# Four fused pre-norm layers on one core: the last block's convolution wholly on TensorE, transposes of h moved within six frames, and a scatter issued later

## The chip, the cores and the metric

The kernel runs on one core of a Trainium2 chip. The metric is device time in microseconds for one execution. Before the change the median of 3 runs is 1512.05 us (1512.02 to 1517.49).

The engines are named as in the profile: PE is TensorE (PEld its weight loads), DVE is VectorE, ACT is ScalarE, POOL is GpSimd, SP is the engine that issues most transfers. Each runs its own instructions in program order; they wait for one another through semaphores.

## The reference, cut to what matters

The input x has 8 blocks of 512 rows of 128 numbers, all fp32. Four layers follow one another, each adding an attention part and a feed-forward part, and every part reads the layernorm of x:

```python
for part in (L0_attn, L0_ffn, L1_attn, L1_ffn, L2_attn, L2_ffn, L3_attn, L3_ffn):
    x = x + part(layernorm(x), weights)
```

The change touches the tail of layer 1's feed-forward part and what comes after. In layer 1, 256 chosen rows go through one expert of eight; their result is put back to their places (in the kernel, by a scatter into a tensor `back` in memory, and for block 0 by a product with a one-hot matrix). Layer 2 is attention with 16 heads of 64 over the 512 rows of each block, and then, for the first two blocks only, low-rank experts. Layer 3 is

```python
def L3_attn(x):                       # 21 taps per channel, causal
    c = sum(table[i] * shifted(x, i) for i in range(1, 21))   # table[0] is 0
    return x @ W1 + c @ W2 + bias
def L3_ffn(x):
    q = lambda a: fp4_round(a / scale(a)) * scale(a)   # scale by blocks of 16
    h = silu(q(x) @ q(w_gate).T) * (q(x) @ q(w_up).T)  # 352 wide
    return q(h) @ q(w_down).T
```

## The kernel before, in words

The residual x stays on chip, one tile of 128 partitions x 4 x 128 per block. The order of instructions on every engine is written out by hand (`manual_schedule`); the tile framework only adds the waits.

**The seam of layers 1 and 2.** `layer1` ends with a list of calls (lines 1178 to 1254). `chosen_out` makes `val`, the result of the chosen rows; `chosen_back` (line 1128) issues two indirect DMAs on POOL's queue that scatter `val` into `back`. The normalisations next to it, `z_stats(7)` and `stats_of(x[0])`, each end with three POOL instructions: add epsilon (line 243), power -1/2 (line 244), and the product with the mean (line 708). `z_out_by_three` adds a product to the residual on POOL (line 956) through one buffer `zo`. `xn` is layer 2's first normalised block; four transposes and a copy make `xt` of it, and `queries(0)` (line 1462) reads that. `keep_clock(n)` (line 765) issues n products that nobody reads.

**Frames.** `late` runs 64 frames, 8 to a block; frame n is two heads of layer 2's attention. In the main loop (line 2014) a frame is: `scores(n, 0)` (two tiles of products of k and q, their maxima on DVE, exponentials on ACT), `context(n - 1)`, `scores(n, 1)`, `queries(n + 2)`, `output(n - 1)`, `values(n + 1)`. Work of other layers hangs in the frames through four hooks: "P" after the first tile's exponentials of `scores(n, 0)` and, on PE, ahead of `context`; "V" just after; "G" between the halves; "E" at the frame's end. `planned(b, f0)` lays layer 3 of block b over 16 frames, from frame 8b + 8 (9 more than 8b for the first two blocks). Its parts are the convolution (`conv_v` on DVE, `conv_s` on ACT and POOL, `join`, then `conv_out` on PE), a second normalisation, the fp4 rounding of x (`quant_x1`, `quant_x2`), `turn_x`, the gate and up products (`gated`) with the rest of silu on DVE (`gated_v`), the rounding of h (`quant_h1`, `quant_h2`), its transposes (`turn_h`) and `down`. `turn_h(0)` hangs in "E", `turn_h(1)` a frame later in "P".

**PSUM.** Eight banks: two pairs (tag "two", used by scores), one each for contexts ("c") and the attention's output ("o"), and two single ones (tag "one") that queries, transposes, convolutions and `down` take in turn. A bank is taken again only when its last reader is done.

**The end.** The last block, 7, has no frames of layer 2 to hide in. `end` (line 1916) writes out an order of its own: block 6 (L) is finished from `gated` on, and block 7 goes through layer 3 in two halves of 256 rows, A and B. Of their 20 taps 12 are done on PE by products with `tap_w`, W2 with its rows scaled by one tap; taps 13 to 16 are on DVE and 17 to 20 on ACT and POOL. The weights `tap_w` are made by ACT, one per frame, in hook "G" from frame 25 on (line 1911). The two roundings of h share one buffer each for scale and values.

Of the kernel before, what the change touches and what calls it, by code (L numbers as in the profile page):

```python
# [160 lines left out]
def body(ctx, tc, dram, spans, x_in, ib, it, ic, ei, out):  # L161
# [84 lines left out]
    def mm(out_, lhs, rhs, start=True, stop=True):  # L246
        nc.tensor.matmul(out_, lhs, rhs, start=start, stop=stop)  # L247
# [534 lines left out]
    def layer1():  # L782
# [9 lines left out]
        with tc.tile_pool(name="l1", bufs=2) as wp, tc.tile_pool(name="l1c", bufs=1) as once:  # L792
# [145 lines left out]
            def z_turn(b):  # L938
                z_turned(t[b]["zn"], b % 2, J)
# [219 lines left out]
            with tc.manual_schedule():  # L1159

                nc.scalar.activation(
                    stat.tile([P, J], F32, tag="nb", name="nb")[:, :1], half[:, :1], AF.Exp
                )
                for zt in zts:
                    nc.gpsimd.memset(zt[64:65, :], 1.0)
                nought = once.tile([P, J, D], F32, tag="nought", name="nought")
                nc.gpsimd.memset(nought, 0.0)
                for b in range(1, NB):
                    nc.sync.dma_start(
                        back[b * TB : (b + 1) * TB, :].rearrange("(j p) d -> p j d", p=P), nought  # L1170
                    )
# [194 lines left out]
    def late():  # L1366
# [11 lines left out]
        with tc.tile_pool(name="a2", bufs=2) as wp, tc.tile_pool(name="l3", bufs=1) as lp:  # L1378
# [252 lines left out]

            pad = 20

            turned_taps = tuple(range(1, 13))
            tap_w = {}

            def tap_weights():
                w = lp.tile([P, 4, TB], F32, tag="cg", name="tapw")
                for k, i in enumerate(turned_taps):
                    tap_w[i] = w[:, k // 4, (k % 4) * P : (k % 4 + 1) * P]  # L1640
# [21 lines left out]
            def layer3(b, xp, tile_, part=(0, J), conv_bank="one", h_tag="h"):  # L1662
# [37 lines left out]
                def conv_p(*taps):  # L1700

                    t["conv"] = ps = bank(conv_bank)
                    for j in range(j0, j1):
                        for i in (0, *taps):
                            mm(
                                cols(ps, j),
                                xp()[:, pad - i + j * P : pad - i + (j + 1) * P],
                                tap_w[i] if i else l3["w1"],
                                start=(j == j0 and i == 0),
                                stop=False,  # L1710
                            )

                def join():
                    nc.vector.tensor_tensor(t["acc"], t["acc"], t["acs"], ALU.add)
# [44 lines left out]
                def gated(j):  # L1759

                    h = tile_("h", h_tile)
                    if whole:
                        pg, pu = bank(), bank()
                    else:
                        two = bank2()
                        pg, pu = two[:, 0, :], two[:, 1, :]
                    mm(pg[:, :I3], cols(t["xt"], j - j0), wt["gate"])
                    mm(pu[:, :I3], cols(t["xt"], j - j0), wt["up"])
                    s = lp.tile([P, I3], F32, tag="s", name="s", bufs=2)
                    nc.scalar.activation(s, pg[:, :I3], AF.Tanh, scale=0.5)  # L1770

                    def rest():
                        nc.vector.scalar_tensor_tensor(s, s, 1.0, pg[:, :I3], ALU.add, ALU.mult)
                        nc.vector.scalar_tensor_tensor(
                            h[:, j, :], s, 0.5, pu[:, :I3], ALU.mult, ALU.mult
                        )

                    t["rest", j] = rest

# [59 lines left out]
            def planned(b, f0_):  # L1839
# [26 lines left out]
                for j in range(J):  # L1866
# [49 lines left out]
            def end():  # L1916
# [14 lines left out]
                L.gated(0)  # L1931
                A.scale()
                L.gated_v(0)
                A.turn_()
                L.gated(1)
                B.scale()
                L.gated_v(1)
                B.turn_()
                L.gated(2)
                A.conv_p(*turned_taps)  # L1940
                A.conv_v(*range(13, 17))
                A.conv_s(*range(17, 21))
                L.gated_v(2)
                L.gated(3)
                B.conv_p(*turned_taps)
                L.quant_h1(0)
                B.conv_v(*range(13, 17))
                B.conv_s(*range(17, 21))
                A.join()
                A.conv_out()  # L1950
                A.stats2()
                L.gated_v(3)
                L.quant_h2(0)
                B.join()
                A.scale2()
                B.conv_out()
                B.stats2()
                A.quant_x1()
                A.quant_x2()
                L.turn_h(0)  # L1960
                B.scale2()
                L.quant_h1(1)
                A.turn_x()
                A.gated(0)
                A.gated(1)
                B.quant_x1()
                B.quant_x2()
                A.gated_v(0)
                A.gated_v(1)
                B.turn_x()  # L1970
                L.quant_h2(1)
                A.quant_h1(0)
                B.gated(2)
                B.gated(3)
                B.gated_v(2)
                A.quant_h2(0)
                L.turn_h(1)
                B.gated_v(3)
                L.down()
# [4 lines left out]
                A.down()  # L1984
                B.turn_h(1)
                B.down()

# [89 lines left out]
```

## Time and profile before

| | us |
|---|---|
| median of 3 runs | 1512.05 |
| the profiled execution | 1515.83 |
| its span, first to last instruction | 1514.0 |
| first scores of frame 0 | 560.44 |
| scores of frame 63 | 1427.34 |
| last add of the end | 1510.50 |

A frame is 11.12 to 16.75 us long, without experts; a block of 8 frames takes 103.04 us in the middle of the run. In an answer of the timeline, a line gives start, duration, engine, source line, operation, tiles (out<-in), shapes and count; "[0.42 <-DVE k L1471]" says that the engine was idle for 0.42 us just before, and what ended it. Durations of instructions in a pipeline overlap a little. PEclk is the granted clock of TensorE as a share of full speed.

### The profile page before, as it was taken

The page shows a single profiled execution, that of the slowest core. Times are in us where ns is not written, and L with a number is a line of the kernel's source. Part 1 is how long each engine was busy: PE and PEld are TensorE (multiplying, and loading weights), DVE is VectorE, ACT ScalarE, POOL GpSimd, SP SyncE. Part 2 cuts the span into 40 slices and gives each one's busy share as a digit, 9 for nine tenths or more (in the row PEclk, how much of TensorE's full clock was granted, in tenths as well). Part 3 has the DMA queues.
Part 4 walks back from the last instruction along what each step waited for, and adds up shares of the span by engine and source line. Part 5 has one row for each costly group of instructions (what it writes and reads, how often), then busy time and mean ns, then how long its engine had stood idle before and what let it go on. Part 6 is the DMA issues. An engine that isn't in the chain of part 4 may idle for free.

```text
span 1514.0 us, 22178 instructions
## 1 busy us (share of the span) xinstructions
PE 1408.5 (93%) x7670; PEld 671.8 (44%) x7670; DVE 1004.4 (66%) x2087; ACT 1049.5 (69%) x2141; POOL 648.3 (43%) x752
## 2 busy tenths in 40 slices
PE   7789999998789989999999999999999999999975
PEld 3652222222367654443443445445444444454554
DVE  6776777767466526552673486786777777867857
ACT  6869999888767446664875575876866767767621
POOL 6647666665655332310530172452532533514432
PEclk9999999999999799999999999999999999999986
DMA  5049999977331010001000000000000000000000
GB/s 181 1 60 133 130 126 129 129 116 102 86 132 32 15 39 22 22 0 27 2 1 1 0 1 8 1 2 7 1 1 8 1 8 1 1 8 1 1 7 15
DMA packets 32898, 58.90 MB, mean 39 GB/s; under 512 B 5522, under 2 KB 25554, under 8 KB 28307
## 3 DMA queue, kind: packets, MB, share of 16 engines
q1 hardware_dynamic: 32080, 55.66, 21.4%
q10 hardware_dynamic: 578, 1.57, 0.3%
q8 instruction: 61, 1.00, 0.3%
q14 instruction: 51, 0.41, 0.1%
q0 software_dynamic: 128, 0.26, 0.1%
HBM read 49.18 MB, written 8.29 MB: 38 GB/s over the span
## 4 chain that ended last, share of the span: by engine, by line
PE 65%; ACT 13%; DVE 13%; DMA 4%; POOL 2%; issue 2%; SPq 0%; POOLq 0%; DVEq 0%; ACTq 0%
PE ps L247 62%; ACT hm L556 4%; ACT ex L1498 3%; DMA gs<-gates 2%; ACT hm L555 2%; DVE nm L1492 2%; DMA gates<-eq 1%; DVE pr L568 1%; POOL rs L244 1%; DVE s L1402 1%; DVE fm L1299 1%; DVE fa L1300 1%; DVE fa L1301 1%; DVE s L703 1%; ACT xn L714 1%
## 5 line engine op out<-in xcount | busy, mean ns | idle before, releaser
L1498 ACT ACTIVATE ex<-ps,nm 128x512 f32<-128x512 f32 x512 | 345.4, 686 | 189.0 <-DVE nm L1492 182.2
L1492 DVE TENSOR_REDUCE nm<-ps 128x2 f32<-128x1024 f32 x256 | 300.4, 1215 | 71.4 <-PE ps L247 71.4
L247 PE MATMUL ps<-q,k 64*128 64x512 f32 x1024 | 256.7, 617 | 5.4 <-ACT ex L1498 4.5
L247 PE MATMUL ps<-ex,vs 128*64 128x512 f32 x1024 | 233.8, 599 | 0.0
L574 POOL TENSOR_TENSOR acc<-acc,pr 128x512 f32<-128x512 f32 x119 | 166.1, 1396 | 108.6 <-DVE pr L568 103.3
L1513 POOL TENSOR_TENSOR vs<-v,sm 128x256 f32<-128x256 f32 x128 | 81.3, 635 | 306.0 <-DVE sm L1512 283.0
L556 ACT ACTIVATE hm<-ps,blob_f 128x1536 f32<-128x1536 f32 x128 | 196.3, 1533 | 0.0
L247 PE MATMUL ps<-xt,blob_a 128*128 128x512 f32 x304 | 152.8, 629 | 0.0
L247 PE MATMUL ps<-h,w 32*128 32x512 f32 x1024 | 148.0, 639 | 3.4 <-DVE eq L467 1.8
L247 PEld LDWEIGHTS ps<-q,k 64*128 64x128 f32 x1024 | 87.2, 186 | 136.8 <-issue 67.8
L247 PE MATMUL ps<-hm,w 128*32 128x512 f32 x1024 | 136.4, 605 | 11.6 <-DVE pr L568 10.8
L568 DVE SCALAR_TENSOR_TENSOR pr<-ps,blob_f,gs 128x512 f32<-128x512 f32 x120 | 89.8, 748 | 73.8 <-PE ps L247 58.7
L1698 POOL TENSOR_TENSOR acs<-acs,prod 128x512 f32<-128x512 f32 (+1 forms) x104 | 128.9, 1240 | 16.7 <-ACT prod L1697 11.9
L247 PEld LDWEIGHTS ps<-ex,vs 128*64 128x64 f32 x1024 | 67.9, 136 | 151.9 <-issue 133.8
L555 ACT ACTIVATE hm<-ps,blob_f 128x512 f32<-128x512 f32 x128 | 88.0, 687 | 29.4 <-PE ps L247 29.3
L1498 ACT ACTIVATION_READ_ACCUMULATOR ex<-ps,nm 128x1 f32 x512 | 104.4, 204 | 0.0
L243 POOL TENSOR_SCALAR rs<-mv 128x4 f32<-128x4 f32 (+1 forms) x69 | 17.6, 254 | 202.5 <-DVE mv L1404 142.5
L247 PEld LDWEIGHTS ps<-xt,blob_a 128*128 128x128 f32 x304 | 53.3, 194 | 87.6 <-issue 66.5
L247 PEld LDWEIGHTS ps<-h,w 32*128 32x128 f32 x1024 | 40.9, 183 | 111.6 <-ACT hm L555 86.1
L1460 DVE TENSOR_TENSOR v<-ps,blob_bc 128x512 f32<-128x512 f32 x64 | 44.2, 690 | 65.8 <-PE ps L247 42.7
L247 PEld LDWEIGHTS ps<-blob_a,ct 128*128 128x128 f32 x512 | 67.0, 192 | 32.3 <-issue 29.2
L244 POOL TENSOR_TENSOR rs<-rs,half 128x4 f32<-128x4 f32 (+1 forms) x69 | 72.3, 1047 | 5.8
(295 smaller groups left out, 2230.3 us busy)
## 6 DMA issues: line engine op xcount, KB each, us to landing
gs<-gates SPq DMA_DIRECT2D x256, 128.0 KB
blob_f<-in_f SPq DMA_DIRECT2D x1, 2560.0 KB
blob_a<-in_a SPq DMA_DIRECT2D x1, 2056.0 KB
x<-in_x SPq DMA_DIRECT2D x8, 256.0 KB
gates<-eq SPq DMA_DIRECT2D x8, 256.0 KB
by_rows<-fxn SPq DMA_DIRECT2D x8, 256.0 KB
ge<-gates SPq DMA_DIRECT2D x4, 512.0 KB
back<-nought SPq DMA_DIRECT2D x7, 256.0 KB
```

Of the source, the lines that this page charges most:

```text
L243: nc.gpsimd.tensor_scalar(t, var, EPS, None, ALU.add)
L244: nc.gpsimd.tensor_tensor(t, t, half[:, : t.shape[-1]], ALU.pow)
L247: nc.tensor.matmul(out_, lhs, rhs, start=start, stop=stop)
L555: nc.scalar.activation(hm[:, 0, :], p1, AF.Gelu, bias=bias)
L556: nc.scalar.activation(hm[:, 1:, :], p3, AF.Gelu, bias=bias)
L568: nc.vector.scalar_tensor_tensor(pr, po, f0["b2"][:, e : e + 1], gs, ALU.add, ALU.mult)
L574: nc.gpsimd.tensor_tensor(acc[:, b, :], acc[:, b, :], pr, ALU.add)
L1460: nc.vector.tensor_tensor(v, pv, bias, ALU.add)
L1492: nc.vector.tensor_reduce(nm, ps, AX.X, ALU.max, negate=True)
L1498: nc.scalar.activation(ex[kt][:, i, :], ps[:, i, :], AF.Exp, bias=nm[:, i : i + 1], accum_out=sm[:, kt, i : i + 1],)
L1513: nc.gpsimd.tensor_tensor(vs[:, tiles, :, :], vs_[n][:, tiles, :].rearrange("p j (i n) -> p j i n", i=2), sm[:, tiles, :].unsqueeze(3).to_ ...
L1698: nc.gpsimd.tensor_tensor(t["acs"], t["acs"], p, ALU.add)
```

## The change

Five things are altered.

1. In `layer1`, `chosen_back()` is called after `stats_of(x[0])` and no longer before `z_stats(7)`.
2. `turn_h(0)` hangs in hook "P" of its frame, and no longer in "E". This concerns six blocks, 0 to 5; block 6's frames after the last one are dropped in favour of `end`.
3. `turned_taps` has all 20 taps. Eight more weights are made by ACT, in frames 37 to 44, in a new tile `tapx` (the last four).
4. In `end`, `conv_tile` does all taps and the W1 product of one tile of 128 rows in a row on PE, 21 products a tile; `conv_v`, `conv_s`, `join` and `conv_out` aren't called there any more. The order of `end` is new, with three `keep_clock`.
5. In `gated` for A and B, ACT copies half of the up product to SBUF, and POOL makes the last product of h from it; L's still runs on DVE. L's gate and up products take a "two" pair in `end`.

```diff
                 chosen_out()
-                chosen_back()
                 z_stats(7)
...
                 by = stats_of(x[0], J)
+                chosen_back()
                 z_turn(6)
...
-            turned_taps = tuple(range(1, 13))
+            turned_taps = tuple(range(1, 21))
...
+                def conv_tile(j):
+
+                    if j == j0:
+                        t["conv"] = bank(conv_bank)
+                    for i in (0, *turned_taps):
+                        mm(
+                            cols(t["conv"], j),
+                            xp()[:, pad - i + j * P : pad - i + (j + 1) * P],
+                            tap_w[i] if i else l3["w1"],
+                            start=(j == j0 and i == 0),
+                            stop=(j == j1 - 1 and i == turned_taps[-1]),
+                        )
...
+                    if at_end and thirds:
+                        u = block("prod", 3)()[:, :I3]
+                        nc.scalar.activation(u, pu[:, :I3], AF.Copy, scale=0.5)
...
+                        if at_end and thirds:
+                            nc.gpsimd.tensor_tensor(h[:, j, :], s, u, ALU.mult)
...
-                    (z + 5, "E", lambda: s.turn_h(0)),
+                    (z + 5, "P", lambda: s.turn_h(0)),
```

The order of calls in `end` after the two `stats`, before and after (g is `gated`, gv `gated_v`, kc `keep_clock`):

```
before: L.g0 A.scale L.gv0 A.turn_ L.g1 B.scale L.gv1 B.turn_ L.g2 A.conv_p A.conv_v A.conv_s L.gv2 L.g3
        B.conv_p L.quant_h1(0) B.conv_v B.conv_s A.join A.conv_out A.stats2 L.gv3 L.quant_h2(0) B.join
        A.scale2 B.conv_out B.stats2 A.quant_x1 A.quant_x2 L.turn_h(0) B.scale2 L.quant_h1(1) A.turn_x
        A.g0 A.g1 B.quant_x1 B.quant_x2 A.gv0 A.gv1 B.turn_x L.quant_h2(1) A.quant_h1 B.g2 B.g3 B.gv2
        A.quant_h2 L.turn_h(1) B.gv3 L.down B.quant_h1 A.turn_h B.quant_h2 (two tiles) A.down B.turn_h B.down
after:  L.g0 L.g1 A.scale A.turn_ L.gv0 B.scale L.g2 L.gv1 B.turn_ L.g3 A.conv_tile x2 L.quant_h1(0) L.gv2
        L.quant_h2(0) L.gv3 L.quant_h1(1) A.conv_added A.stats2 L.turn_h(0) L.quant_h2(1) B.conv_tile x2
        A.scale2 A.quant_x1 A.quant_x2 B.conv_added B.stats2 A.turn_x A.g0 B.scale2 A.g1 L.turn_h(1) A.gv0
        B.quant_x1 A.gv1 B.quant_x2 L.down kc6 B.turn_x B.g2 B.g3 A.quant_h1 A.quant_h2 B.gv2 B.gv3 kc8
        B.quant_h1 A.turn_h B.quant_h2 (two tiles) A.down kc6 B.turn_h B.down
```

More of the change, by code (lines that the diff above doesn't have):

```diff
@@ L1638, in tap_weights @@
                 w = lp.tile([P, 4, TB], F32, tag="cg", name="tapw")
+                more = lp.tile([P, TB], F32, tag="tapx", name="tapx")
                 for k, i in enumerate(turned_taps):
-                    tap_w[i] = w[:, k // 4, (k % 4) * P : (k % 4 + 1) * P]
+                    part = w[:, k // 4, :] if k < 16 else more
+                    tap_w[i] = cols(part, k % 4)
                     yield lambda i=i: nc.scalar.activation(
@@ L1698, in conv_s, with conv_p, conv_added @@
                             nc.gpsimd.tensor_tensor(t["acs"], t["acs"], p, ALU.add)
-                def conv_p(*taps):
+                def conv_p():
                     t["conv"] = ps = bank(conv_bank)
                     for j in range(j0, j1):
[L1704 to L1711, printed above, removed]
+                        mm(
+                            cols(ps, j),
+                            xp()[:, pad + j * P : pad + (j + 1) * P],
+                            l3["w1"],
+                            start=(j == j0),
+                            stop=False,
+                        )
[3 more added lines that the diff above has]
+                    for i in (0, *turned_taps):
+                        mm(
+                            cols(t["conv"], j),
[3 more added lines that the diff above has]
+                            stop=(j == j1 - 1 and i == turned_taps[-1]),
+                        )
+                def conv_added():
+                    added(t["conv"])
                 def join():
@@ L1757, in h_tile, with gated @@
                     return flat[:, : J * I3].rearrange("p (j i) -> p j i", j=J)
-                def gated(j):
+                def gated(j, at_end=False, thirds=True):
                     h = tile_("h", h_tile)
-                    if whole:
+                    if not at_end:
                         pg, pu = bank(), bank()
@@ L1770, in gated @@
                     nc.scalar.activation(s, pg[:, :I3], AF.Tanh, scale=0.5)
+                    if at_end and thirds:
+                        u = block("prod", 3)()[:, :I3]
+                        nc.scalar.activation(u, pu[:, :I3], AF.Copy, scale=0.5)
                     def rest():
                         nc.vector.scalar_tensor_tensor(s, s, 1.0, pg[:, :I3], ALU.add, ALU.mult)
-                        nc.vector.scalar_tensor_tensor(
-                            h[:, j, :], s, 0.5, pu[:, :I3], ALU.mult, ALU.mult
-                        )
+                        if at_end and thirds:
+                            nc.gpsimd.tensor_tensor(h[:, j, :], s, u, ALU.mult)
+                        else:
+                            nc.vector.scalar_tensor_tensor(
+                                h[:, j, :], s, 0.5, pu[:, :I3], ALU.mult, ALU.mult
+                            )
                     t["rest", j] = rest
@@ L1930, in end @@
                     h.stats()
-                L.gated(0)
+                L.gated(0, True, False)
+                L.gated(1, True, False)
                 A.scale()
+                A.turn_()
                 L.gated_v(0)
-                A.turn_()
-                L.gated(1)
                 B.scale()
+                L.gated(2, True, False)
                 L.gated_v(1)
                 B.turn_()
-                L.gated(2)
-                A.conv_p(*turned_taps)
-                A.conv_v(*range(13, 17))
@@ L1942, in end @@
-                A.conv_s(*range(17, 21))
+                L.gated(3, True, False)
+                A.conv_tile(0)
+                A.conv_tile(1)
+                L.quant_h1(0)
                 L.gated_v(2)
[L1944 to L1950, printed above, removed]
+                L.quant_h2(0)
+                L.gated_v(3)
@@ L1951, in end @@
+                L.quant_h1(1)
+                A.conv_added()
                 A.stats2()
-                L.gated_v(3)
-                L.quant_h2(0)
-                B.join()
+                L.turn_h(0)
+                L.quant_h2(1)
+                B.conv_tile(2)
+                B.conv_tile(3)
                 A.scale2()
-                B.conv_out()
-                B.stats2()
                 A.quant_x1()
                 A.quant_x2()
-                L.turn_h(0)
+                B.conv_added()
@@ L1961, in end @@
+                B.stats2()
+                A.turn_x()
+                A.gated(0, True)
                 B.scale2()
[L1962 to L1965, printed above, removed]
+                A.gated(1, True)
+                L.turn_h(1)
+                A.gated_v(0)
                 B.quant_x1()
+                A.gated_v(1)
                 B.quant_x2()
-                A.gated_v(0)
-                A.gated_v(1)
+                L.down()
@@ L1970, in end @@
+                keep_clock(6)
                 B.turn_x()
-                L.quant_h2(1)
+                B.gated(2, True)
+                B.gated(3, True)
                 A.quant_h1(0)
-                B.gated(2)
-                B.gated(3)
+                A.quant_h2(0)
                 B.gated_v(2)
-                A.quant_h2(0)
-                L.turn_h(1)
                 B.gated_v(3)
-                L.down()
+                keep_clock(8)
                 B.quant_h1(1)
@@ L1984, in end @@
                 A.down()
+                keep_clock(6)
                 B.turn_h(1)
```

## The prediction, made blind

> **What bounds the kernel now.** I read the page first. Its engine rows and its slices say TensorE nearly everywhere, with a few thin places:
>
> ```profile
> span 1514.0 us, 22178 instructions
> ...
> PE 1408.5 (93%) x7670; PEld 671.8 (44%) x7670; DVE 1004.4 (66%) x2087; ACT 1049.5 (69%) x2141; POOL 648.3 (43%) x752
> ...
> PE   7789999998789989999999999999999999999975
> ```
>
> TensorE is at 9 tenths through layer 2 and drops at the very end. All three edits act where it is not fully busy, so each needs its own timeline. First TensorE in the frame at 1109.90, the one with `turn_h(0)` of block 2:
>
> ```profile
> 1120.03 1.06 PE L247 MATMUL ps<-blob_a,xt 128*128 128x128 f32 x8
> 1121.51 0.55 PE L1805 MATMUL ps<-blob_c,h 128*128 128x128 f32 x3 [0.42 <-DVE k L1471]
> 1123.11 0.55 PE L1805 MATMUL ps<-blob_c,h 128*128 128x128 f32 x3 [1.06 <-ACT q L1470]
> 1123.59 1.99 PE L247 MATMUL ps<-q,k 64*128 64x512 f32 x8
> 1125.51 0.87 PE L1805 MATMUL ps<-blob_c,h 128*128 128x128 f32 x6
> ```
>
> The reader should see that the two transposes of h wait 0.42 + 1.06 us for the two "one" banks, which `queries` has just filled and which k on VectorE and q on ScalarE empty late. The last line is `turn_h(1)` a frame later, already placed between scores and context: all six transposes in 0.87, no wait. That is what the edit makes of the first kind.
>
> Second, POOL at the seam of layers 1 and 2:
>
> ```profile
> 540.73 1.11 POOL L1130 DMA_INDIRECT back<-val,at_int  x1 [7.12 <-DVE s L703]
> 543.38 0.96 POOL L1130 DMA_INDIRECT back<-val,at_int  x1 [1.55 <-DMA back<-val,at_int]
> 544.36 0.26 POOL L243 TENSOR_SCALAR rs<-mv 128x4 f32<-128x4 f32 x1
> ...
> 547.21 0.23 POOL L243 TENSOR_SCALAR rs<-mv 128x4 f32<-128x4 f32 x1
> ```
>
> The second scatter waits for the first to land, and the deviations of z(7) and then of x(0) queue behind it. The chain of waits of this stretch runs through both to `xn` of layer 2 at 548.87.
>
> Third, VectorE and POOL at the end, from 1468 on:
>
> ```profile
> 1472.59 0.89 DVE L1301 TENSOR_TENSOR fa<-fa,fm 128x704 f32<-128x704 f32 x1
> 1473.40 0.42 DVE L1714 TENSOR_TENSOR acc<-acc,acs 128x256 f32<-128x256 f32 x1
> 1475.14 0.42 DVE L1717 TENSOR_TENSOR x<-x,ps 128x256 f32<-128x256 f32 x1 [1.31 <-PE ps L247]
> ...
> 1491.48 0.89 DVE L1280 TENSOR_REDUCE fsc<-h 128x44 f32<-128x704 f32 x1 [1.50 <-POOL h L1302]
> ...
> 1504.15 0.81 DVE L1299 TENSOR_SCALAR fm<-fm 128x352 f32<-128x352 f32 x1
> ...
> 1510.50 0.42 DVE L1717 TENSOR_TENSOR x<-x,ps 128x256 f32<-128x256 f32 x1 [4.09 <-PE ps L247]
> ```
>
> From 1475 to 1506 VectorE is the bound (idle about 2 us in all), while it idled 7.25 us before 1468.30, waiting for the convolution. B's `join` at 1473.40 stands behind L's rounding, and TensorE waited 5.62 us for it.
>
> **The transposes, in six frames.** Counted from the end of `values` to the next frame's scores. Frames of blocks 1, 2, 3: 2.50 (1121.09 to 1123.59) becomes 0.80 for six transposes in a row, -1.70 each. Block 0 (frame at 899.31): waits of 0.90 + 1.06; afterwards the convolution behind them takes that bank and can start only when k is read, at 911.39 as the transposes do now; with its 1.98 the frame ends at 913.4 and not 915.38, so -2.0. Block 4: one wait of 0.42, 1.40 becomes 0.80: -0.6. Block 5 has no queries after it and no wait: nothing gained on TensorE. Sum -7.7.
> What it costs: four copies of ht (0.83 together at 1332.21 to 1333.04) now stand in front of the second tile's exponentials on ScalarE. Queued behind them are ct, xn and the third tile's exponentials. Where those wait for VectorE anyway the copies are hidden: ScalarE idled 1.61 us there for block 2, 4.1 for block 0. In block 5's frame it idled only
>
> ```profile
> 1425.80 0.69 ACT L1498 ACTIVATE ex<-ps,nm 128x512 f32<-128x512 f32 x1 [0.32 <-DVE nm L1492]
> ```
>
> so 0.83 - 0.32 = 0.5 is late, and the next frame's scores, which already waited for those exponentials (0.17 at 1428.64), pass it on: +0.5. (Block 4 has as little idle, but its next scores come 0.9 after the bank is free.) Net **-7.2**. Bounds: -8 if block 5 absorbs it, -4.5 if each frame paid the 0.5. VectorE's order in these frames is unchanged.
>
> **Eight more tap weights.** Eight 0.39 us ScalarE copies, one in each of frames 37 to 44. Frames 34 to 36 have one already and last 12.30 us each, as their counterparts 42 to 44 do without: 0. Uncovered they would be 3.1.
>
> **The scatter.** POOL's z(7) chain (0.26 + 1.04 + 0.20) can start at 541.3, when its mv is there, then the residual add of z(5) (1.26), then x(0)'s chain when VectorE has its mv at 545.07: done 546.7 instead of 548.84, -2.1. But the two `keep_clock` bursts hold TensorE to 548.89, so the transposes of xn start there and xt is copied from 549.5, not 550.93: **-1.4**, and the rest of the chain (zn, zt, zo, the last POOL add, qb, q) follows. The two scatters (546.8 to 550.3 on POOL) now delay the adds of z(6) and of "lb"; nobody needs those before z(7)'s add at about 556. SP's first read of the rows comes at 560.25, after the new landing at about 552.8. Here the granted clock was 0.51 from 552.8 to 559.6, with TensorE waiting from 549 on. "TensorE: Matmul & The Clock Gate" of the Trainium skill, in its part on the clock gate, puts the drop down to an idle free-running window of about 3.4 us. By the row the clock still drops (TensorE would do only transposes from 549.5 to 552.7); by the rule that gap is now just under a window, and full clock would let POOL's chain bind instead: q at 556.5 rather than 558.3, -3.2. I take the row; -3.2 and 0 are the bounds.
>
> **The end.** I list the end's instructions in program order with the rows' durations and waits. For the order of before this gives the last add at 1510.15 against 1510.92 in the trace, 0.8 short, so only differences are used.
> TensorE: each half's convolution is 2 x 21 products instead of 2 x 13 + 2 acc products: 0.2225 us each at full clock, 9.35 us. A runs 1454.7 to 1464.1, L's transposes 0.8, B to 1474.3. In the trace B's convolution was added at 1475.14: -0.9, because B no longer waits for `join`.
> VectorE from that add to its last rounding took 30.5 us (1475.56 to 1506.08). Out of this stretch go A's quantisation of x (2.9), L's scale (2.5) and rounding (2.9) with the POOL wait (1.5), now in the gap under the convolutions, and four multiplications for h (4 x 0.52), now on POOL: -11.9. Into it come B's deviations and xn (1474.7 to 1477.8; +2.2 of idle) and POOL: A's h (1.39) and then two of B's products, about 0.87 each by the 128x352 row at 1503.89, hold B's scale back from 1489.2 to 1491.5 (+2.3). -7.4. Sum with -0.9: -8.3; the list gives -7.7 (same cold clock after 1490).
> "GPSIMD Engine Reference", section on engine selection, speaks against giving POOL such products: about twice VectorE's time for two inputs. The row says 0.87 against 0.52, 1.7 times; twice would be 1.04, +0.3 over the two. And the 0.81 at 1504.15 against 0.34 for its twin at 1502.28 shows VectorE held while POOL multiplies (1503.89 to 1504.76); once, in B's rounding of x, that falls on the path: +0.5.
> L's gate and up products now take two-bank tiles, which are free by then (their last exponentials end at 1439.6): 0. `keep_clock` adds 20 products (4.5 us): six before B's `turn_x`, which then starts at 1483.6 and not 1482.2; VectorE is in A's h until 1488, so 0. Last steps after the final POOL product (PE, copy, PE, add) stay about 4. Net **-7.2**, bounds -9 and -4.5 (another 3 us of half clock or a slower POOL).
>
> **Sum.** -7.2 - 1.4 - 7.2 = -15.8. The profiled execution took 1515.83 (span 1514.0), giving 1500.0. The median shown, 1512.05, is 3.8 lower; the same difference gives **1496.2**.
>
> **Rivals.**
> 1. *The end gives nothing*: POOL's products and the serial TensorE order (A's `turn_x` stands behind B's whole convolution, 1471.9 to 1474.2) become the wait. For: POOL already ends VectorE's waits there. Against: VectorE has 12 us less between. 1512.05 - 7.2 - 1.4 = 1503.5. Chance 0.15.
> 2. *The transposes buy nothing*: the copies move the wait to the score banks. For: 0.32 of idle in one frame. Against: `turn_h(1)` runs so without a wait in four frames. -8.6 alone: also 1503.5; with half the end gone 1507. Chance 0.11.
> 3. *Slower*: the clock. If TensorE got half clock through the whole end, the list's end comes 17.4 later instead of 7.7 earlier: 1512.05 - 8.6 + 17.4 = 1520.9. It decides once the end loses more than 8.6. Against: the granted clock was 1.00 from 1454 to 1468, and there is more to do now. Chance 0.04.
> The forecast, 1490 to 1501: 0.70. Range 1490 to 1504. About 0.5% (7.6 us) is what a measurement here tells from no change; below 1504.5 is faster: 0.87, within 0.10, slower 0.03.
>
> **What would show it.** Right: no wait before the six-in-a-row transposes; the block period shorter by 1.7 (103.0 to 101.3); xn of layer 2 at 546.8 with its transposes after the clock-keeping products; B's convolution added about 9.5 us earlier (7.2 + 1.4 from ahead of it, 0.9 of its own); VectorE waiting for `POOL h` before B's scale. Wrong: scores waiting for `ACT ex` in those frames; clock 0.5 under the convolutions.

## The result and the profile after

The median after is 1494.85 us (1492.55 to 1503.02, 5 runs) against 1513.1 before (1512.02 to 1517.49, 5 runs). The ratio is 0.9884, 95% interval 0.9852 to 0.9916, or -17.6 us (-12.7 to -22.4). Forecast were 1496.2 and -15.8. The profiled execution took 1492.55, with a span of 1490.8:

```profile
span 1490.8 us, 22351 instructions
...
PE 1405.8 (94%) x7766; PEld 674.7 (45%) x7766; DVE 1000.3 (67%) x2073; ACT 1049.2 (70%) x2145; POOL 648.2 (43%) x750
...
PE   7789999988879889999999999999999999999996
```

These lines don't say which edit did what, and TensorE's digits hardly differ. The stages do say it. I cut each trace at five marks that both kernels have: the product with `put` near the end of layer 1, the first scores of frame 0, of frame 1 and of frame 62, and A's add at the start of the end (its first read of the attention's output).

| stage, us | before | after | difference | forecast |
|---|---|---|---|---|
| start to `put` | 540.90 | 534.31 | -6.6 | 0 |
| `put` to frame 1 | 30.31 | 30.43 | +0.1 | -1.4 |
| frame 1 to frame 62 | 846.07 | 838.32 | -7.75 | -7.7 |
| frame 62 to A's add | 29.16 | 29.58 | +0.4 | +0.5 |
| A's add to the last add | 64.48 | 55.00 | -9.5 | -7.2 |

The span became 23.2 us shorter, 6.6 of it ahead of anything that was changed. The last section comes back to that. The changed stages give -16.7.

**The transposes.** TensorE in the frame with `turn_h(0)` of block 2, which answers to the frame at 1109.90 before:

```profile
1099.70 1.99 PE L247 MATMUL ps<-q,k 64*128 64x512 f32 x8
1101.62 0.87 PE L1828 MATMUL ps<-blob_c,h 128*128 128x128 f32 x6
1102.42 3.65 PE L247 MATMUL ps<-ex,vs 128*64 128x512 f32 x16
```

Six transposes in 0.87 us, between scores and context, with no wait. Frame 22 lasts 14.07 (16.07 before), frames 30, 38 and 46 11.92 (13.69), frame 54 11.92 (12.41), frame 62 10.44 (10.06, less than the 11.12 given above as the shortest frame, as is frame 0 with 10.77). Apart from frame 0, all others are as before, so the period of eight frames is 101.27 (103.04).

**The seam.** POOL:

```profile
538.57 0.25 POOL L243 TENSOR_SCALAR rs<-mv 128x4 f32<-128x4 f32 x1 [0.98 <-DVE mv L705]
...
540.38 1.11 POOL L1130 DMA_INDIRECT back<-val,at_int  x1 [0.16 <-issue]
543.44 0.96 POOL L1130 DMA_INDIRECT back<-val,at_int  x1 [1.95 <-DMA back<-val,at_int]
```

x(0)'s chain now waits for VectorE's mv and for nothing else, and the wait of the second scatter (1.55 before, 1.95 now) stands behind it. The first scores come 17.86 after `put` instead of 19.54. But frame 0 then lasts 12.58 instead of 10.77, and the gain is gone.

**The end.** VectorE:

```profile
1458.82 0.42 DVE L1734 TENSOR_TENSOR x<-x,ps 128x256 f32<-128x256 f32 x1 [1.99 <-PE ps L247]
...
1464.78 0.93 DVE L1299 TENSOR_SCALAR fm<-fm 128x256 f32<-128x256 f32 x1
...
1472.67 0.95 DVE L1793 SCALAR_TENSOR_TENSOR s<-s,ps 128x352 f32<-128x352 f32 x2
1476.09 0.89 DVE L1280 TENSOR_REDUCE fsc<-h 128x44 f32<-128x704 f32 x1 [2.48 <-POOL h L1795]
...
1487.22 0.42 DVE L1734 TENSOR_TENSOR x<-x,ps 128x256 f32<-128x256 f32 x1 [4.09 <-PE ps L247]
```

B's convolution is added 26.18 us after A's first add (28.70 before). From there to the add that follows the last rounding it takes 23.90 (30.86), and then 4.92 (4.92) to the end of the last add. In the middle VectorE waits 2.48 us for POOL, which makes A's rounded h and then two of B's products. POOL, in the same stretch:

```profile
1472.90 1.39 POOL L1302 TENSOR_TENSOR h<-fa,fsc 128x704 f32<-128x704 f32 x1 [4.06 <-DVE fa L1301]
1474.24 1.82 POOL L1795 TENSOR_TENSOR h<-s,prod 128x352 f32<-128x352 f32 x2
```

### The profile page after: what moved, and what is told of

It is laid out like the page before. It is cut to its first block, busy times and chain, and to the rows that moved or that the text cites. A ratio compares the mean times of both kernels' runs of the same rounds, so it can differ in the third digit from the quotient of the medians.

```text
span 1490.8 us, 22351 instructions
## 1 busy us (share of the span) xinstructions
PE 1405.8 (94%) x7766; PEld 674.7 (45%) x7766; DVE 1000.3 (67%) x2073; ACT 1049.2 (70%) x2145; POOL 648.2 (43%) x750
## 4 chain that ended last, share of the span: by engine, by line
PE 71%; ACT 14%; DVE 10%; POOL 2%; issue 2%; DMA 1%; POOLq 0%; DVEq 0%; ACTq 0%
PE ps L247 68%; ACT hm L556 6%; ACT hm L555 3%; ACT ex L1498 2%; DVE pr L568 1%; DVE nm L1492 1%; ACT xn L1414 1%; POOL rs L244 1%; DVE s L703 1%; PE ps L1828 1%; DVE frc L1282 1%; ACT xn L714 1%; ACT h L377 0%; DVE fm L1299 0%; PE ps L929 0%
## 5 line engine op out<-in xcount | busy, mean ns | idle before, releaser
L1700 POOL TENSOR_TENSOR acs<-acs,prod 128x512 f32<-128x512 f32 x98 | 124.8, 1273 | 10.7 <-ACT prod L1699 6.1
```

## The experiments

My theory is that of the forecast: the three edits act in three places, the frames through banks, the seam through POOL's queue, the end through VectorE's load. The main rival is TensorE's clock: that the end got shorter because twenty-one products in a row hold the clock at full, and that sums over whole runs are blurred by it. All stages below are read from each run's own trace. e4 to e7 and e10 to e12 were run once each (1495.35, 1494.6, 1492.72 and 1491.34 us; 1494.89, 1516.72 and 1490.8), so of them only the stages are used. A window is a stretch of 3.41 us: in all these traces the half clock (a granted clock of 0.50) comes in multiples of it. A burst is one call of `keep_clock`. "`put` to frame 1", "1 to 62", and the three parts of the end (A's add to B's convolution added, from there to the add after the last rounding, tail) are:

| run | to scores of 0 | frame 0 | 1 to 62 | frame 62 | end in three parts | end |
|---|---|---|---|---|---|---|
| before | 19.54 | 10.77 | 846.07 | 10.06 | 28.70 + 30.86 + 4.92 | 64.48 |
| after | 17.86 | 12.58 | 838.32 | 10.44 | 26.18 + 23.90 + 4.92 | 55.00 |
| e1 only the transposes | 19.44 | 10.77 | 838.28 | 10.43 | 27.92 + 31.72 + 4.92 | 64.56 |
| e2 only the scatter | 17.86 | 12.44 | 849.32 | 10.06 | 28.64 + 30.59 + 4.05 | 63.28 |
| e3 only the end | 19.15 | 10.78 | 848.87 | 10.05 | 26.18 + 23.89 + 4.92 | 54.99 |
| e4 no clock-keeping in the end | 17.86 | 12.57 | 838.27 | 10.43 | 26.18 + 23.89 + 4.92 | 54.99 |
| e5 B's h on VectorE | 17.00 | 10.77 | 838.28 | 10.43 | 26.18 + 22.62 + 3.40 | 52.20 |
| e6 more clock-keeping | 17.86 | 12.44 | 838.27 | 10.43 | 26.17 + 23.90 + 3.40 | 53.47 |
| e7 seam, later products | 15.90 | 10.77 | 838.28 | 10.43 | 26.18 + 23.89 + 4.92 | 54.99 |
| e8 three things | 17.85 | 12.68 | 838.31 | 10.06 | 26.18 + 22.63 + 3.54 | 52.35 |
| e9 e7 and e8 | 15.91 | 10.78 | 838.31 | 10.06 | 26.18 + 22.62 + 3.54 | 52.34 |
| e10 old scatter, later products | 17.95 | 12.41 | 838.32 | 10.44 | 26.18 + 23.91 + 4.92 | 55.01 |
| e11 before, end clocked | 19.14 | 10.78 | 848.83 | 10.06 | 31.91 + 30.30 + 3.40 | 65.61 |
| e12 all of h on VectorE | 17.85 | 12.64 | 838.31 | 10.44 | 26.18 + 22.45 + 4.93 | 53.56 |

### One edit at a time: e1, e2, e3

e1 is the kernel before with one line of the change:

```diff
-                    (z + 5, "E", lambda: s.turn_h(0)),
+                    (z + 5, "P", lambda: s.turn_h(0)),
```

e2 is the kernel before with the scatter moved:

```diff
                 chosen_out()
-                chosen_back()
                 z_stats(7)
...
                 by = stats_of(x[0], J)
+                chosen_back()
```

e3 is the changed kernel with both of these undone.

> The kernel before with the six turn_h(0) in P alone; nothing is left out. My theory: in the stretch from the first scores of frame 1 to those of frame 62 each of the three frames of blocks 1 to 3 is 1.7 to 1.8 us shorter, block 0's 2.0, block 4's 0.5, so -7.7; frame 62 is 0.4 to 0.5 longer; the ends, from A's first added on, take 64.5 us as before (63 to 65, by where the half-clock stretches fall). Time: about 7 us under the kernel before. Rival (the frames got shorter because the tap weights or the clock changed, not the transposes): the frames last 13.7 as before and the time is within 2 us. Second rival, a difference between executions: frames other than 22, 30, 38, 46, 54 and 62 change too.

Measured: ratio 0.9937 (0.99 to 0.9974), -9.5 us. Frames 1 to 62 take 838.28, frame 62 10.43, no other frame but the six moves by 0.05. The theory holds by stages; the -9.5 has more in it than their -7.4, within its interval.

> The kernel before with chosen_back moved behind the statistics of x[0] alone; nothing is left out. My theory of the seam: from the put product to the first scores of frame 0 it takes 17.9 us instead of 19.5 (-1.7), because POOL reaches x(0)'s chain 2 us earlier; whether that is kept at the first scores of frame 1 (30.3 us after the put product before) depends on the half-clock stretch in frame 0: 28.6 if it is 6.8 us as before, 30.4 if it is 10.2. Time 0 to -1.7, not to be told from none. Rival (the scatter's place does not matter, TensorE's clock-keeping products set xn's transposes): 19.5 to the scores of frame 0. Frames 1 to 62 stay at 846.1, the end at 64.5. Up to the put product, where nothing differs from before and after, I expect a spread of several us between traces (540.9 in before, 534.3 in after), all of it in the time at half clock.

Measured: ratio 0.9998 (0.9984 to 1.0011), no difference. The first scores come at 17.86, frame 0 lasts 12.44, together 30.30: the branch with the longer half clock. One thing I hadn't expected: frames 1 to 62 take 849.32 and not 846.1, because frames 22 and 39 are 1.52 and 1.66 longer. TensorE in the frame of block 2's transposes, in e2:

```profile
1114.10 0.55 PE L1805 MATMUL ps<-blob_c,h 128*128 128x128 f32 x3 [0.42 <-DVE k L1471]
1115.71 0.55 PE L1805 MATMUL ps<-blob_c,h 128*128 128x128 f32 x3 [1.06 <-ACT q L1470]
1116.18 3.65 PE L247 MATMUL ps<-q,k 64*128 64x512 f32 x8
```

The waits are those of before, 0.42 and 1.06, but the eight score products behind them take 3.65 us and not 1.99. The granted clock (the column after the engines' busy times) in two stretches of 3.41 us:

```profile
1112.95:1116.36 3.41, 1.92 (x15) 1.30 (x15) 1.86 (x4) 3.18 (x12) 0.75 (x2) 1.00 0.00 0
1116.36:1119.77 3.41, 3.41 (x9) 0.90 (x9) 1.23 (x1) 0.75 (x3) 0.00 (x0) 0.50 0.00 0
```

TensorE was busy for 1.92 of 3.41 us, and then had half clock for 3.41. In the profiled execution of before the same waits fell otherwise, and the clock stayed. How long TensorE is busy doesn't decide it alone: in frame 30 of e2 the same two waits fell into the window 1010.55 to 1013.97, also with 1.93 us of work, and the clock stayed at 1.00. What tells the two windows apart is open.

> The end of the changed kernel alone: turn_h(0) is back in E and the scatter at its old place; nothing is left out. My theory: from A's added to the last add 55 to 57 us, against 64.5 before and 55.0 in the whole change; frames 1 to 62 take 846.1 as before, the seam 19.5. Of the 9.5 us, 7 to 7.5 are the order and about 2 the clock: if the stretch to B's convolution added takes 28.0 instead of 26.2 in this execution, it has a half-clock stretch in it. Time -7 to -9.5. Rival (the end is shorter because of what comes earlier, its clock in above all): 60 us or more.

Measured: ratio 0.9946 (0.9928 to 0.9964), -8.2 us. The end takes 54.99, whatever came ahead of it. The three ratios multiplied give 0.9881, the whole change 0.9884: within their intervals, the edits add up. Frames 22 and 47 have half clock here too (+1.13 and +1.64).

### What the end's gain is made of: e4, e11, e5, e12, e6

e4 is the changed kernel without the three `keep_clock` of `end`:

```diff
-                keep_clock(6)
                 B.turn_x()
...
-                keep_clock(8)
                 B.quant_h1(1)
...
-                keep_clock(6)
                 B.turn_h(1)
```

> The whole change without the 20 clock-keeping products in the end; they take no part in what is computed. My theory: VectorE is the bound there, so its stretch from B's convolution added to the last rounding stays at 24.0 us within 0.5; TensorE falls to half clock one or two windows (3.4 to 6.8 us) earlier than at 1480.6, which costs the transposes and gate products of B some tenths; the end takes 55.0 to 56. Rival (the gain in the end comes from the clock that those products keep): the end takes 58 or more.

Measured: 54.99, to 0.01 the end with those products, although TensorE falls to half clock 41.4 us after A's add, and in the changed kernel only 48.2 us after it; in both it stays there to the last product. The 20 clock-keeping products of the new end buy nothing. The rival falls: VectorE's work sets the pace.

e11 is the kernel before with such products in its own `end`:

```diff
+                keep_clock(8)
                 A.turn_()
...
+                keep_clock(24)
                 B.conv_out()
...
+                keep_clock(14)
                 A.turn_x()
...
+                keep_clock(10)
                 L.turn_h(1)
...
+                keep_clock(10)
                 A.turn_h(0)
...
+                keep_clock(12)
                 B.turn_h(1)
```

> The kernel before with clock-keeping products in the idle stretches of TensorE in its end (8 before A's transposes, 24 before B's last convolution products, 14 before A's turn_x, 10 before L's second transposes, 10 before A's, 12 before B's); nothing is left out. It tells how much of the end's 9.5 us is order and how much clock. My theory: TensorE at full clock saves the order of before 2 to 3 us, so its end takes 61 to 62.5 us instead of 63.3 to 64.6, and the order keeps 6.5 to 7.5 of the 9.5. Rival (all is order, VectorE sets the pace in both): 63.3 or more. Other rival (most is clock): below 60.

Measured: 65.61, outside the 61 to 62.5 of my theory, but the total is spoilt by the bursts themselves. TensorE in e11:

```profile
1449.30 2.80 PE L247 MATMUL ps<-blob_c 128*128 128x128 f32 x16 [1.95 <-DVE s L1773]
...
1472.00 5.62 PE L247 MATMUL ps<-blob_c 128*128 128x128 f32 x48 [1.88 <-DVE s L1773]
```

The burst takes a bank like any other, so it waited 1.95 and 1.88 us for `gated_v` to release one and then stood in front of A's transposes and B's last convolution products: the first part grew to 31.91. As a test of the whole sum the run is inconclusive. Behind it, with full clock throughout, the VectorE part (B's convolution added to the add after the last rounding) took 30.30, against 30.59 to 31.72 in the three traces of the old order with half clock. So full clock is worth 0.3 to 1.4 us there, and the order 30.30 - 23.90 = 6.4.

e5 is the changed kernel with B's products for h on VectorE; e12 does the same to `A.gated(0)` and `A.gated(1)` as well:

```diff
-                B.gated(2, True)
-                B.gated(3, True)
+                B.gated(2, True, False)
+                B.gated(3, True, False)
```

> The whole change with B's two products for h back on VectorE (0.52 each) instead of POOL (0.93 each, and two ScalarE copies of 0.46); nothing is left out. My theory: VectorE's wait of 2.48 us for POOL's second product goes and 1.04 us of work comes, so B's convolution added to the last rounding takes 22.5 to 22.7 instead of 24.0, the end 53.6. Rival (the wait is for the chain from B's xt through the gate product, not for POOL): the stretch stays at 24.0 or grows to 25.

Measured: the second part 22.62, -1.28 against after. The theory holds: POOL's products cost more than they take off VectorE. The tail is 3.40 and not 4.92 besides, which I hadn't expected: TensorE's wait before its last transposes fell from 3.03 to 1.76 us, and the clock stayed at full. TensorE in e5:

```profile
1485.11 0.55 PE L1828 MATMUL ps<-blob_c,h 128*128 128x128 f32 x3 [1.76 <-POOL h L1302]
```

That the shorter wait kept the clock is not shown by this one trace: in e12 the wait is 2.12 us, and the clock falls.

> The changed kernel with A's and B's four products for h on VectorE; nothing is left out. It tells what POOL's two products for A are worth alone, against B's on VectorE (end 52.2 us). Theory: A's two add 1.04 us to VectorE's path, less about 0.8 of rounding instructions no longer held while POOL multiplies, so 52.2 to 53.2. Rival (POOL's products hold VectorE as long as they free it): 51.5 to 52.2.

Measured: the second part 22.45, so A's two products on POOL were worth nothing either (-0.17 more without them); my 1.04 less 0.8 had the wrong sign, the rival is right in that part. The end as a whole is 53.56, above both ranges of the expectation, because the tail is back at 4.93. VectorE in e12, first in the rounding of B's x and then at B's scale:

```profile
1464.73 0.29 DVE L1299 TENSOR_SCALAR fm<-fm 128x256 f32<-128x256 f32 x1
...
1474.35 0.89 DVE L1280 TENSOR_REDUCE fsc<-h 128x44 f32<-128x704 f32 x1 [0.46 <-DVE h L1797]
```

The first line took 0.93 in the changed kernel, where POOL multiplied at the same time; the wait of 2.48 before the second is 0.46.

e6 is the changed kernel with a longer last burst:

```diff
-                keep_clock(6)
+                keep_clock(20)
                 B.turn_h(1)
```

> The whole change with 20 instead of 6 clock-keeping products ahead of B's last transposes, where TensorE waits 3.03 us for POOL; nothing is left out. The 14 more take 3.1 us at full clock. My theory: the granted clock stays at 1.00 up to the end, the last twelve down products take 1.4 instead of 2.8 us, and the tail from the last rounding (4.84 us) 3.3 to 3.5. Rival (the products lie ahead of the transposes and delay them, or the clock drops anyway): the tail stays at 4.8 or grows by up to 1.5.

Measured: the tail is 3.40. TensorE in e6, and below it in the changed kernel:

```profile
1478.70 4.63 PE L247 MATMUL ps<-blob_c 128*128 128x128 f32 x40
1483.48 0.52 PE L1828 MATMUL ps<-blob_c,h 128*128 128x128 f32 x3
...
1485.80 1.56 PE L247 MATMUL ps<-wd,ht 128*128 128x128 f32 x12
```

```profile
1481.54 0.90 PE L1828 MATMUL ps<-blob_c,h 128*128 128x128 f32 x3 [3.03 <-POOL h L1302]
...
1484.42 2.77 PE L247 MATMUL ps<-wd,ht 128*128 128x128 f32 x12
```

The extra products fill the wait of 3.03 us and don't lie on the path; the last twelve instructions take 1.56 instead of 2.77, the transposes above them 0.52 instead of 0.90. The theory holds, and so clock-keeping is worth 1.5 us in that one place. It isn't one execution's luck: with the 20 products e8 and e9 have a tail of 3.54, and with 6 or none every trace of the new end but e5 has 4.92 or 4.93.

### Where the seam's gain went: e7, e10

e7 is the changed kernel with the seam's second burst later; e10 is e7 with `chosen_back()` at its old place:

```diff
-                keep_clock(6)
                 t[0]["next"] = turned(norm, "xt", xn)
                 z_scale(7)
+                keep_clock(6)
                 z_turn(7)
+                keep_clock(4)
                 z_out_by_three(7)
```

The changed kernel, TensorE in frame 0 and its stretches of 3.41 us ahead of it:

```profile
547.77 3.62 PE L247 MATMUL ps<-xt,blob_a 128*128 128x512 f32 x4
552.17 3.79 PE L247 MATMUL ps<-q,k 64*128 64x512 f32 x8 [0.78 <-ACT q L1470]
```

```profile
541.98:545.40 3.42, 1.95 (x11) 0.95 (x10) 0.00 (x0) 2.24 (x6) 1.94 (x2) 1.00 0.12 38
545.40:548.81 3.41, 2.91 (x10) 2.39 (x11) 0.00 (x0) 1.19 (x4) 1.52 (x2) 0.53 0.00 0
548.81:552.22 3.41, 2.63 (x6) 0.54 (x4) 0.82 (x2) 1.09 (x3) 1.26 (x1) 0.50 0.02 8
552.22:555.63 3.41, 3.41 (x8) 1.13 (x8) 1.22 (x1) 0.08 (x1) 0.00 (x0) 0.50 0.68 183
```

The clock itself changes 0.2 us after these marks, at 545.60 and at 555.84. Cut there, the window ahead of the drop has 1.75 us of work (mostly the transposes of xn and zn), and then the clock is at half for three windows. It comes back only after the one that TensorE filled, up to 555.84, and that one lies in frame 0: its first scores take 3.79 and not 1.99. Before the change the filled window was 556.09 to 559.50, just ahead of frame 0 at 560.44. By starting the frame sooner, the change puts the last 3.4 us at half clock into it.

> The whole change with the second clock-keeping burst of the seam (6 products) moved behind the transposes of xn, and 4 more ahead of the output of z(7); nothing is left out. My theory: the transposes of xn start at once behind xn (about 540.8 instead of 542.1 on the changed kernel's scale), and TensorE has work in the window in which the clock dropped to half, so frame 0 lasts about 10.8 us and not 12.6, and from the put product to frame 1 it takes 27.5 to 29 instead of 30.4. Rival (the clock drops there whatever, because the waits for zt and zo are longer than the products): frame 0 keeps 12.6 and the stretch 29.5 to 30.5.

Measured: 26.67, better than forecast. The clock is 1.00 throughout, the scores come at 15.90, frame 0 lasts 10.77.

> The changed kernel with the later clock-keeping products of the seam, but with the second scatter at its old place; nothing is left out. If the scatter's place is worth about 2 us once the clock holds, the stretch from the put product to frame 1 takes 28.2 to 29 us here, against 26.7 with the scatter moved. If the clock alone made that stretch shorter, and the scatter's place is nothing, it takes 26.7 here too. If the longer wait for xn lets the clock fall in spite of the products, 30 or more.

Measured: 30.36. TensorE in e10:

```profile
545.24 1.48 PE L736 MATMUL ps<-blob_c,xn 128*128 128x128 f32 x4 [1.88 <-ACT xn L714]
...
554.67 3.30 PE L247 MATMUL ps<-q,k 64*128 64x512 f32 x8 [1.20 <-ACT q L1471]
```

With the scatter at its old place the transposes of xn wait 1.88 us, and the scores come at 17.95, 2.05 later than in e7: that is what the scatter's place is worth. The clock then fell in frame 0, and the third branch of the expectation came true. By frame 1 the later products alone gave nothing in e10 (30.36), both edits together 3.7 us (26.67 and, in e9, 26.69). The scatter alone depends on how the windows fall. The old order takes 29.92 to 30.31 in its four traces (before, e1, e3, e11), and six of the seven traces with only the scatter moved take 30.29 to 30.53. The seventh, e5, takes 27.77: its clock was at half for one window only, 553.79 to 557.20, ahead of its scores at 558.88. So the scatter alone is worth 2.1 to 2.5 us in such an execution and nothing in the others; with the later products both traces have that gain and 1.1 us more. Whether the clock falls in e10 however the windows fall, one trace can't tell.

### Versions that go further: e8, e9

e8 is after with e5, e6 and `turn_h(0)` of block 5 back in "E"; e9 has e7 as well.

> The whole change with three things: B's products for h on VectorE, 20 clock-keeping products ahead of the last transposes, and turn_h(0) of the last planned block (frame 62) back in E; nothing is left out. Theory: -1.4, -1.4 and -0.4 us, -3.2 in all against the changed kernel, so about 1491.7 in the median and a ratio to before of .986. By stage: frame 62 lasts 10.1 instead of 10.4, B's convolution added to the last rounding 22.6, the tail 3.4. Rival (what the end gains is taken by the clock): the end stays at 54.5 to 55.

Measured: 1492.24 (1489.51 to 1496.41, 6 runs), ratio 0.9842 (0.9813 to 0.9871). Frame 62 is at 10.06 again, the end 52.35: -3.0 against after by stages (forecast -3.2). That is -0.38 in frame 62, -1.27 in the second part and -1.38 in the tail; the tail's gain is the one that e5 and e6 both had, and counts once.

> The whole change with four more things: the later clock-keeping products of the seam, B's products for h on VectorE, 20 clock-keeping products ahead of the last transposes, turn_h(0) back in E for the block of frame 62; nothing is left out. Theory, by stages that earlier traces gave alone: from the put product to frame 1 26.7 us (30.4 in the changed kernel, -3.8), frame 62 10.06 (-0.4), the end 52.3 (-2.7): -6.8 in all against the changed kernel, a ratio to before of .984 to .980, the median about 1488. Rival (the seam's gain is one execution's clock): put to frame 1 stays at 30.3 and the run near 1492.

Measured: the profiled execution took 1486.8, the least of all, with the stages as forecast (26.69, 838.31, 10.06, 52.34). The timed runs don't confirm the gain over e8: median 1492.59 (1486.8 to 1494.14, 4 runs), ratio 0.9866 (0.9842 to 0.989), and both intervals overlap that of the change itself. So e9 beats the changed kernel by 6.8 us in the stages of its one trace, and the times here can't tell it from e8. e12's placement of h together with e6's products (22.45 + 3.4, another 0.3) wasn't tried.

## Why the prediction was right, and where it missed

**The transposes, -7.2: right.** -7.75 + 0.38 = -7.4 in the two traces shown; each frame is within 0.15 of its term, also the one that gets longer (+0.38 against +0.5), and e1 alone shows them. (The lower bound was mis-added: 0.5 in each of six frames leaves -4.7, not -4.5.) What the step left out is the clock: the waits it removes were in three of four traces of the old order also the cause of two windows of half clock, +2.8 to +3.3 us (849.32, 848.87, 848.83 against 846.07). With the new place all ten traces have 838.27 to 838.32. So in these traces the edit is worth 7.4 to 10.6, and I had priced its waits from an execution in which they were cheapest.

**The eight tap weights, 0: right.** In e3, which has the weights and not the moved transposes, frames 37 to 44 last as before.

**The scatter, -1.4: the mechanism was right, the sum wrong.** x(0)'s chain came 2 us sooner and the scores 1.68. The step took from the row "the clock still drops" that the drop costs the same as before, and didn't ask where it ends. It ends in frame 0, in six of seven traces with the scatter moved and the old clock-keeping products (12.44 to 12.68; the seventh, e5, has 10.77), and it costs the 1.7 us that were gained. Measured is +0.1 at frame 1 in the pair shown, against the upper bound of 0; e2's ratio shows no difference either. Only in e5, where the half clock ended ahead of frame 0, was the gain kept. The lower bound, -3.2 with the clock held, is what e7 gave, and more (-3.6 against before).

"TensorE: Matmul & The Clock Gate" of the Trainium skill, in its part on the clock gate, has a free-running window of about 3.4 us, an idle one for the drop and a busy one for the return. The multiples of 3.41 us agree, and in the changed kernel the return after a filled window. Elsewhere the return doesn't follow so simply: in e8 the window 547.40 to 550.81 was filled and the clock stayed at half, in e1 one with 2.73 us of work (563.05 to 566.46) brought it back. The windows that led to a drop here were not idle: 1.92 us of work in e2 and 1.75 in the changed kernel, of 3.41. By the rule as I had read it, a gap "just under a window" was safe; two waits of 0.42 and 1.06 us were enough in e2, and in its frame 30 they were not. So the runs give no threshold, and a forecast from the length of a gap alone could not have been sure.

**The end, -7.2: right in kind, too small.** -9.5 in the pair shown, -8.3 against e2. By terms:
- The convolution, -0.9: -2.52. Of this, 0.78 is a window of half clock that before had at the start of its end and e1 has not (28.70 against 27.92). The rest, -1.74, is the order. The step let A's convolution start where it did, at 1454.7 or 8.3 us after A's add. It starts 6.6 after it (7.6 in e1), because L's second gate products now run in the gap ahead of A's transposes; and B's behind L's transposes as worked out.
- VectorE, -7.4: -6.96, or -6.4 against e11. The waits that the step put into it are there: 2.48 us for POOL (forecast 2.3), and 1.62 and 0.24 behind B's convolution (forecast 2.2 in all).
- The tail, 0: 0.
- That makes -9.5, where the terms worked out by hand gave -8.3 and the list of rows -7.7, to which +0.5 for one held rounding was added. The list carried the half clock of before into the new end; the new end had none from 1424 to 1480. By these traces about 8.1 of the 9.5 is the order (1.74 + 6.4); the other 1.3 (0.78, and 30.86 - 30.30) is half clock that the profiled execution of before happened to have.

**The sum, -15.8 against -16.7 by stages and -17.6 by the ratio.** That it came so close is in part luck: the seam gave 1.5 us less than forecast and the end 2.3 more, and the two errors are opposite.

**POOL's products for h: the sizes right, the sign of the sum not asked.** Forecast: 0.87 each, 2.3 of wait, one held rounding of +0.5, against 2.08 taken off VectorE. Measured: 0.93, 2.48, +0.64 (0.93 against 0.29). The terms as forecast sum to a loss of 0.7 already, and I hadn't set them against each other. Undoing all four gains 1.45 in that part (e12). The estimate from the doubling in the Trainium skill's "GPSIMD Engine Reference", section on engine selection (1.04), and the row (0.87) lay either side of the 0.93, which is 1.8 times VectorE's 0.52.

**The rivals.** "The end gives nothing" and "the transposes buy nothing" fell with e3 and e1. The slow one, by the clock, didn't come about: the clock was full under the convolutions, and in e4 6.8 us more at half clock behind them cost nothing.

## What to carry to other kernels

Price a removed wait on TensorE by the clock windows it can open, not only by its own length, and look at more than one execution for it. If work is moved ahead of a frame, ask where the half-clock stretch ends afterwards; clock-keeping products pay where they fill the very window ahead of products on the critical path (1.5 us at the tail, 3.7 at the seam with the scatter), and nothing where VectorE set the pace (e4). When a slower engine takes over a product, set its wait and its holds against what it saves before calling the move part of the gain.

## What the hardware showed that was not expected

The code up to the `put` product is the same in all fourteen traces, and it takes from 531.92 to 547.13 us. The time goes with the half clock that the trace shows up to there: 20.5 us of it in e2 (531.92), 27.3 in after (534.31), 41.0 in before (540.90), 58.0 in e1 (547.13), about 0.4 us for each us at half clock. The stretch from 480 to 530, in e1:

```profile
480.00:530.00 50.00, 45.71 (x157) 29.11 (x155) 29.14 (x140) 18.98 (x49) 14.45 (x27) 0.65 0.07 19
```

and in e2:

```profile
480.00:530.00 50.00, 44.53 (x238) 31.03 (x237) 33.14 (x153) 28.60 (x73) 19.60 (x34) 0.93 0.07 19
```

TensorE is busy for as long in both, at a mean clock of 0.65 and 0.93, and gets through 157 and 238 products. The 6.6 us of the first table that belong to no edit are of this kind: at 0.4, the 13.7 us of half clock between before and after make some 5.5 of them. The 40 runs of the kernel before taken with e1 to e3 (1507.87 to 1521.4) have no traces, but each has its span and mean granted clock. From these, 63 to 97 us of a run are at half clock, and the time goes with that (correlation 0.97, about 0.43 us for each us). Where in those runs the half clock lies, and what sets it, isn't shown. A single trace's span says nothing about changes of this size. Its stages do, if their half clock is read along with them.
